# A graph network with four transformer layers on one core: three re-orderings around the gated feed-forward stage

## The chip, the cores and the metric

The kernel runs on one core of one Trainium2 chip. Its time is the device time of one execution in microseconds (us); three runs of the kernel before gave 2254.66, 2255.79 and 2258.05, with a median of 2255.79. The profile is that of one more execution. The engines are named as the profile names them: PE (TensorE, with PEld for its weight loads), DVE (VectorE), ACT (ScalarE), POOL (GpSimd) and SP (SyncE, which here issues nearly all DMAs).

## The reference

Node features of 1024 rows by 512 are normalised, passed through a graph convolution, then through four layers of cross attention and a gated feed-forward block, then a second graph convolution. The change touches the feed-forward block alone:

```python
for i in range(L):                                    # L = 4
    a = _attn(_ln(h, ln2_w[i], ln2_b[i]), cond, Wq[i], Wk[i], Wv[i], Wo[i])
    h = h + a
    u = _ln(h, ln3_w[i], ln3_b[i]) @ geglu_w[i] + geglu_b[i]   # 512 -> 4096
    val, gate = jnp.split(u, 2, axis=-1)
    f = val * jax.nn.gelu(gate, approximate=False)             # 1024 x 2048
    h = h + f @ ffo_w[i] + ffo_b[i]                            # 2048 -> 512
h = _gcn(h, src, dst, gcn_out_w, gcn_out_b, n)
return h + x_in
```

## The kernel before

**Numbers in three parts.** [...] A product is then three matmuls for each block of 128 along the inner size: high by high, low by low, and third by third. The high and low products go into a PSUM bank, which is scaled by 1 + TINY, and the third product is added; in the chunks and in `Twelve` an ACT operation scales the bank in place (`g L373`, `g L1157`) between the first two and the third, so a unit has a `begin` (high, low, scaling) and an `end` (third), and other units' matmuls are put between the two.

**The gated block.** f transposed has 2048 rows in sixteen column blocks ("chunks") of 128. The normalised input is kept transposed in the tiles ln3T. The first two columns (`PLAIN = 2`) are computed as plain products in two halves of the rows (`halves`, class `Half`, L1028): the first half while the last attention group is finished, the second half, `half_1(0) + half_1(1)`, at L1891 and below. The other fourteen chunks use seven products of half the size in the place of eight (class `Chunk`, L1093): sums of blocks of the input ("late rows", held in `right`, numbered 5, 6, 4, 3) and sums of blocks of the weight. The late rows are split by the generator `late_parts` (L1871), whose steps the function `fill` takes: for a row first two ACT multiplications (L1863, one for each half of the row), then two steps with two DVE operations each (L1866, L1868). Row 5, 4 and 3 come from the tiles ln3S, row 6 from ln3T. The third step of a row also begins the next row, so the first `fill(3)` goes as far as row 6's multiplications and the second one as far as row 4's first pair of DVE operations.

**The chunk loop.** For each chunk the generator `Chunk.steps` (L1182) emits the products 0, 5, 6, 4, 1, 3, 2 and the additions between them; the endings of products 1, 3 and 2, the gates (ACT, L1172) and the two products of value and gate (DVE, L1223 and L1225) are put in the next chunk's iteration. Beside the chunk in work, the next one's weight blocks are summed on POOL (L1115), and split on ACT, DVE and POOL (L1081, L1082, L1087), and a later one is loaded by SP (L1105). f goes to DRAM (`f_dram`, L1267).

**The output.** `Output` (L1271) multiplies f by ffo_w in two halves of the rows and eight units (`UNITS`) of 256 inner rows each, sixteen units in all, of 24 matmuls (L1322): for four row blocks, two high by high, two low by low (bank fy) and two third by third (bank fx). `fetch(n)` loads a unit's f again and `split(n)` splits it (ah_f L304, al_f L305, as_f L310). `fetch_w(u)` loads a block of ffo_w, and `ahead` is a generator over the splits of all blocks, five steps each: one ACT multiplication (bh_wff, L1296), then for each half of the block a low part (bl_wff, L1299) and a third (bs_wff, L1303) on DVE. In the chunk loop, with n = 0 for the first chunk of the third group of four and n = 7 for the last chunk, the first block is fetched at n = -1 and split in five steps at n = 0 to 4. Each pass of the output loop fetches a unit and a block further on, splits the next unit's f, takes five steps of `ahead`, and emits its own unit's matmuls.

**What sets the order.** The kernel is traced in program order, and a scheduler orders each engine's instructions ahead of the run by its own estimate of times. `pin` keeps the instructions that it is given in program order on their engine, `in_order(engine)` does so for all in a block, and `behind_traced(engine)` ties each instruction of a block behind the last one traced on that engine. At run time each engine takes its instructions in the order thus fixed, and SP its DMAs. A new tile of a pool takes a free buffer; the pool `slots`, from which splits, weights and f come, has 35.

Of the kernel before, what the change touches and what calls it, by code (L numbers as in the profile page):

```python
# [26 lines left out]
def gnn_kernel(  # L27
# [68 lines left out]
    @contextmanager  # L96
    def in_order(engine):

        traced = nc.cur_bb.bb.instructions
        n = len(traced)  # L100
        before = next((i for i in reversed(traced) if i.engine == engine), None)
        yield
        for i in traced[n:]:
            if i.engine == engine:
                if before is not None:
                    tc.add_manual_dep(i, before.name, mybir.DependencyInfo(
                        mybir.DependencyClass.NoSync, mybir.DependencyReason.DATA))
                before = i

    @contextmanager  # L110
    def behind_traced(*engines):

        traced = nc.cur_bb.bb.instructions
        n = len(traced)
        last = {e: next(i for i in reversed(traced) if i.engine == e) for e in engines}
        yield
        for i in traced[n:]:
            if i.engine in last:
                tc.add_manual_dep(i, last[i.engine].name, mybir.DependencyInfo(
                    mybir.DependencyClass.NoSync, mybir.DependencyReason.DATA))  # L120

    def bank(name):
        return psum.tile([P, 512], F32, tag="bank", name=name)
# [168 lines left out]
    def twelve_bits(t):  # L292
        return t.bitcast(F32R)
# [709 lines left out]
    class HalfWeights:  # L1003
# [6 lines left out]
        def load(self, j):  # L1010
            parts = slots_of(3, f"gp_{self.l}_{j}")
            for i, t in enumerate(parts):
                nc.sync.dma_start(self.tall(t), half_dram[j, :, :, i].rearrange("n p f -> p n f"))
            self.parts[j] = [self.tall(t) for t in parts]
# [256 lines left out]
    class Output:  # L1271
# [37 lines left out]
            for u in range(UNITS):  # L1309
                yield from self.split_w(u)  # L1310

        def unit(self, n):

            s, u = divmod(n, UNITS)
            left, right = self.f.pop(n), self.w[u]
            for b in range(4):
                if u == 0:
                    self.banks[b] = [bank(f"{x}_{self.l}_{s}_{b}") for x in ("fy", "fx")]
                y, x = self.banks[b]
                for which, to in enumerate((y, y, x)):  # L1320
                    for k in range(2):
                        pin(nc.tensor.matmul(  # L1322
                            to, twelve_bits(left[which][0])[:, k, b * P:(b + 1) * P],
                            twelve_bits(right[which])[:, k, :],
                            start=u == 0 and which != 1 and k == 0,
                            stop=u == UNITS - 1 and which != 0 and k == 1, skip_group_check=True))
                if u == UNITS - 1:
                    to = h[4 * s + b]
                    nc.vector.scalar_tensor_tensor(to, y, 1.0 + TINY, to, OP.mult, OP.add)
                    nc.vector.tensor_tensor(to, x, to, OP.add)  # L1330
# [164 lines left out]
    for l in range(L):  # L1495
# [147 lines left out]
        def add_bias(t, *blocks):  # L1643
            if not ffb:
                with waiting_for(scores.last, mybir.EngineType.SP):
                    ffb.append(load_row(ffo_b, l * D, f"ffb_{l}"))
            for nb in blocks:
                t.tensor_tensor(h[nb], h[nb], ffb[0], OP.add)
# [85 lines left out]
        def sum_chunk(n):  # L1734
            if n < len(ready):
                ready[n].sums()

        def begin_split(n, low, t=nc.gpsimd):
            flow = ready[n].split_steps(low, t) if n < len(ready) else iter(())
            next(flow, None)  # L1740
            return flow
# [76 lines left out]
        with in_order(mybir.EngineType.DVE):  # L1818
            units = half_0(0) + half_0(1)
            before = oT  # L1820
# [66 lines left out]
        def fill(n=1):  # L1887
            for _ in range(n):
                next(parts, None)
# [3 lines left out]
        ready[0].end_first()  # L1893
        fill(3)
        units[1].begin()
        units[0].end()
        fill(3)
        ready.append(StagedChunk(l, PLAIN + 1))
        units[2].begin()
        units[1].end()  # L1900
# [10 lines left out]
        def split_rest(short, behind=None):  # L1911
            long = begin_split(0, False)
            next(long, None)
            with waiting_for(behind or split_left.low, mybir.EngineType.Pool):
                for flow in short, long:
                    for _ in flow:
                        pass

        output = Output(l)
        ahead = output.ahead()  # L1920
        before, short = None, iter(())
        for r in range(R):
            f = Gated(l, r) if r else f_first
            for c in range(0 if r else PLAIN, KC):
                n = (r - R + 2) * KC + c
                if n == -1:
                    output.fetch_w(0)
                if (r, c) == (R - 1, KC - 2):
                    output.fetch(0)
                chunk = ready.pop(0)  # L1930
                flow = chunk.steps(lambda: sum_chunk(1)) if before else first_flow
                chunk.f = f
                if before:
                    next(flow)
                if 0 < n < 5:
                    next(ahead)
                for _ in islice(short, 2):
                    pass
                if before:
                    next(flow)  # L1940
                the_last = (r, c) == (R - 1, KC - 1)
                if before and r:
                    if not the_last:
                        split_rest(short)
                    load()
                for _ in parts:
                    pass
                if the_last:
                    with in_order(mybir.EngineType.Activation), in_order(mybir.EngineType.DVE), \
                            in_order(mybir.EngineType.Pool):  # L1950
                        output.split(0, nc.gpsimd, lambda: split_rest(short, left_parts.low))
                    output.fetch(1)
                for step in range(3):
                    if before:
                        next(before, None)
                    next(flow)
                    if before and not r and step == 0:
                        split_rest(short)
                        load()
                    if step == 2 and not before:  # L1960
                        with in_order(mybir.EngineType.DVE):
                            add_bias(nc.vector, NG - 2, NG - 1)
                    if step == 1 and not before:
                        ready[0].load_rest()
                        sum_chunk(1)
                        load()
                        with tc.issue_after(ready[-1].loaded.ins):
                            for n in range(PLAIN):
                                f_first.store(n, (1,))
                before = flow  # L1970
                short = begin_split(0, True) if r or c > PLAIN else iter(())
                if n == 0:
                    next(ahead)
        output.fetch_w(1)
        output.fetch_w(2)
        for _ in range(3):
            next(before, None)

        def nothing():
            pass  # L1980
# [22 lines left out]
        else:  # L2003
# [11 lines left out]
            def split_of(to, raw, name, i):  # L2015
                for part, t in zip(to, right_parts(raw[i:i + 1], f"{name}_{l + 1}_{i}")):
                    part.extend(t)
# [16 lines left out]
        with in_order(mybir.EngineType.DVE):  # L2034
            for n in range(2 * UNITS):
                output.fetch(n + 2)
                output.split(n + 1)
                output.fetch_w(n + 3)
                for _ in range(5):
                    next(ahead, None)  # L2040
                output.unit(n)
                beside.get(n, nothing)()
            if not last:
                split_of(wv, raw_wv, "wv", 1)
# [80 lines left out]
```

## Time and profile before

| what | value |
|---|---|
| time, median of three runs | 2255.79 us |
| the profiled execution's own time | 2254.72 us |
| span of the profile | 2252.9 us |
| instructions | 35754 |
| granted TensorE clock | 1.0 |
| busy: PE / DVE / ACT / POOL | 2232.4 / 1718.0 / 1157.8 / 500.5 us |
| moved by DMA | 340.84 MB, mean 151 GB/s |

A busy time is the union of an engine's instructions; as matmuls overlap, a PE that is busy all the time need not run at its full pace. A line of the timeline has its start and duration in us, the engine, the line of the code, the operation, the tile written and those read, shapes, how many equal instructions are merged in it, and in brackets how long the engine had been idle and what released it. In tile names, gr, gl and gs are parts of the late rows (or rights), gha, gla, gsa and ghb, glb, gsb those of a chunk's weights, g the banks. SPq is the queue of SP.

### The profile page before, as it was taken

The numbers are of one execution on the slowest core, as the hardware profiler recorded it, in microseconds if no ns is written. First come the engines' busy times: TensorE is split into PE (matmuls) and PEld (weight loads), VectorE is DVE, ScalarE is ACT, GpSimd is POOL, SyncE is SP. The second block draws the span as 40 slices with busy tenths as digits, with TensorE's granted clock in tenths as the row PEclk, the third lists the DMA queues.
The fourth block names the chain that finished last, engine by engine and source line by source line (L and its number), as shares of the span: only waits on it lengthen the run. The fifth ranks groups of instructions, "written<-read, shape, count | busy, mean of one in ns | idle before, by whom it ended". The sixth has DMA issues, their size and how long they took to land. (4 is left out here: it accounts for less than half of the span.)

```text
span 2252.9 us, 35754 instructions
## 1 busy us (share of the span) xinstructions
PE 2232.4 (99%) x12768; PEld 1805.2 (80%) x12768; DVE 1718.0 (76%) x3300; ACT 1157.8 (51%) x2313; POOL 500.5 (22%) x483
## 2 busy tenths in 40 slices
PE   8999999999999999999999999999999999999999
PEld 4678888887888888888888888888888888888787
DVE  9886677999965567899976466889976466899965
ACT  7555555565354445565346445565436445565521
POOL 1122211386000000287000000178100000068201
PEclk9999999999999999999999999999999999999999
DMA  6154565434425265442534265443543346353551
GB/s 173 58 187 169 189 217 172 144 122 145 165 84 197 99 227 174 150 126 97 196 122 157 106 219 193 132 136 99 187 159 136 127 165 213 110 168 113 187 182 53
DMA packets 216953, 340.84 MB, mean 151 GB/s; under 512 B 16488, under 2 KB 117168, under 8 KB 216768
## 3 DMA queue, kind: packets, MB, share of 16 engines
q1 hardware_dynamic: 214672, 333.05, 43.5%
q0 software_dynamic: 1376, 4.30, 0.6%
q8 instruction: 105, 1.72, 0.3%
q10 hardware_dynamic: 720, 1.11, 0.1%
q14 instruction: 80, 0.66, 0.1%
HBM read 236.69 MB, written 101.72 MB: 150 GB/s over the span
## 5 line engine op out<-in xcount | busy, mean ns | idle before, releaser
L1157 ACT ACTIVATE g<-g 128x512 f32<-128x512 f32 x224 | 131.3, 586 | 183.9 <-PE g L1143 181.9
L1615 POOL TENSOR_TENSOR ln3T<-ln3T,ln3T 128x512 f32<-128x512 f32 x8 | 13.2, 1654 | 875.2 <-DVE ln3S L1608 875.2
L1322 PE MATMUL fx<-bs_wff,as_f 128*128 128x512 f32 x512 | 158.7, 390 | 0.0
L1322 PE MATMUL fy<-bl_wff,al_f 128*128 128x512 f32 x512 | 158.7, 390 | 0.0
L1322 PE MATMUL fy<-bh_wff,ah_f 128*128 128x512 f32 x512 | 157.7, 389 | 0.0
L304 ACT ACTIVATE ah_f<-fr 128x1024 fp32r<-128x1024 f32 x64 | 67.8, 1060 | 172.5 <-DVE al_f L305 80.4
L373 ACT ACTIVATE k<-k 128x512 f32<-128x512 f32 x125 | 73.1, 586 | 153.6 <-PE k L362 153.6
L832 DVE TENSOR_REDUCE nmax<-sc 128x2 f32<-128x512 f32 x128 | 83.7, 678 | 79.6 <-PE sc L823 79.5
L843 ACT ACTIVATE pr<-sc,nmax 128x256 f32<-128x256 f32 x256 | 118.4, 473 | 41.0 <-DVE nmax L832 40.9
L373 ACT ACTIVATE v<-v 128x512 f32<-128x512 f32 x127 | 74.8, 589 | 115.8 <-PE v L362 115.6
L1087 POOL TENSOR_TENSOR gsa<-gha,gla 128x512 fp32r<-128x512 f32 x96 | 122.5, 1299 | 21.4 <-DVE gla L1082 21.4
L1143 PE MATMUL g<-gr,gha 128*128 128x512 f32 x384 | 118.3, 389 | 0.0
L1322 PEld LDWEIGHTS fy<-bl_wff,al_f 128*128 128x128 f32 x512 | 96.1, 188 | 21.5 <-DVE bl_wff L1299 1.7
L1322 PEld LDWEIGHTS fx<-bs_wff,as_f 128*128 128x128 f32 x512 | 96.1, 188 | 21.4 <-DVE bs_wff L1303 1.7
L1322 PEld LDWEIGHTS fy<-bh_wff,ah_f 128*128 128x128 f32 x512 | 96.1, 188 | 19.9
L362 PE MATMUL v<-bh_wv,ch 128*128 128x512 f32 x384 | 106.7, 399 | 0.0
L362 PE MATMUL k<-ch,bh_wk 128*128 128x512 f32 x384 | 104.0, 393 | 0.0
L305 DVE SCALAR_TENSOR_TENSOR al_f<-ah_f,fr 128x1024 fp32r<-128x1024 f32 x64 | 78.1, 1221 | 33.6 <-ACT ah_f L304 27.5
L362 PE MATMUL v<-bl_wv,cl 128*128 128x512 f32 x384 | 103.1, 390 | 0.0
L362 PE MATMUL v<-bs_wv,cs 128*128 128x512 f32 x384 | 103.0, 391 | 0.0
L362 PE MATMUL k<-cl,bl_wk 128*128 128x512 f32 x384 | 102.8, 389 | 0.0
L362 PE MATMUL k<-cs,bs_wk 128*128 128x512 f32 x384 | 101.4, 395 | 0.0
(334 smaller groups left out, 5938.0 us busy)
## 6 DMA issues: line engine op xcount, KB each, us to landing
f_dram<-fT SPq DMA_DIRECT2D x128, 256.0 KB, 2.1
fr<-f_dram SPq DMA_DIRECT2D x64, 512.0 KB, 4.6
ch<-cond_dram SPq DMA_DIRECT2D x48, 512.0 KB, 4.8
cl<-cond_dram SPq DMA_DIRECT2D x48, 512.0 KB, 6.4
cs<-cond_dram SPq DMA_DIRECT2D x48, 512.0 KB, 7.5
chunk_dram<-gs SPq DMA_DIRECT2D x56, 384.0 KB, 2.5
wff<-in_L_gnn_ffo_w_dram SPq DMA_DIRECT2D x32, 512.0 KB, 5.0
half_dram<-gs SPq DMA_DIRECT2D x32, 384.0 KB, 3.5
```

The costliest lines, as they stand in the source:

```text
L304: nc.scalar.mul(twelve_bits(h), x, INWARD * TINY)
L305: left_parts.low = nc.vector.scalar_tensor_tensor(twelve_bits(l), h, -1.0 / TINY, x, OP.mult, OP.add)
L362: pin(nc.tensor.matmul(self.bank, twelve_bits(left[k // 2])[:, k % 2, self.c * P:(self.c + 1) * P], twelve_bits(right[k // 2])[:, k % 2, : ...
L373: nc.scalar.mul(self.bank, self.bank, 1.0 + TINY)
L832: nc.vector.tensor_reduce(nmax[u], banks[u].rearrange("p (a m) -> p a m", a=2), AX.X, OP.max, negate=True)
L843: nc.scalar.activation(pr3[:, a, :], ps3[:, a, :], AF.Exp, bias=nmax[u][:, a:a + 1], accum_out=tot[:, a:a + 1])
L1087: split_left.last = pin(t.tensor_tensor(s_at, h_at, l_at, OP.subtract))
L1143: pin(nc.tensor.matmul(to, self.part(i, which)[:, k, :], self.rights[i][which].bitcast(F32R)[:, k, :], start=start and k == 0, stop=stop a ...
L1157: pin(nc.scalar.mul(to, to, 1.0 + TINY))
L1322: pin(nc.tensor.matmul(to, twelve_bits(left[which][0])[:, k, b * P:(b + 1) * P], twelve_bits(right[which])[:, k, :], start=u == 0 and whic ...
L1615: t.tensor_tensor(b12, b22, b12, OP.subtract)
```

## The change

There are three edits. First, the second `fill(3)` of the late rows is traced before the ending of the second half's first unit, and its ACT instructions are tied behind the last ACT instruction traced before, the scaling of unit 1. Second, the second block of ffo_w is fetched at n = 4, and three of its five steps of splitting are taken at n = 5, 6 and 7; the output loop then always is three steps further in `ahead`. Third, `unit` becomes a generator `products` that stops twice in its first row block, and of unit 0 the high and the low products of the first row block (four matmuls) are emitted after the last chunk's ending of product 1 and before its endings of products 3 and 2.

```diff
--- before.py
+++ after.py
@@ -1309,7 +1309,7 @@
             for u in range(UNITS):
                 yield from self.split_w(u)
 
-        def unit(self, n):
+        def products(self, n):
 
             s, u = divmod(n, UNITS)
             left, right = self.f.pop(n), self.w[u]
@@ -1318,6 +1318,8 @@
                     self.banks[b] = [bank(f"{x}_{self.l}_{s}_{b}") for x in ("fy", "fx")]
                 y, x = self.banks[b]
                 for which, to in enumerate((y, y, x)):
+                    if which:
+                        yield
                     for k in range(2):
                         pin(nc.tensor.matmul(
                             to, twelve_bits(left[which][0])[:, k, b * P:(b + 1) * P],
@@ -1893,8 +1895,9 @@
         ready[0].end_first()
         fill(3)
         units[1].begin()
+        with behind_traced(mybir.EngineType.Activation):
+            fill(3)
         units[0].end()
-        fill(3)
         ready.append(StagedChunk(l, PLAIN + 1))
         units[2].begin()
         units[1].end()
@@ -1925,6 +1928,8 @@
                 n = (r - R + 2) * KC + c
                 if n == -1:
                     output.fetch_w(0)
+                if n == 4:
+                    output.fetch_w(1)
                 if (r, c) == (R - 1, KC - 2):
                     output.fetch(0)
                 chunk = ready.pop(0)
@@ -1932,7 +1937,7 @@
                 chunk.f = f
                 if before:
                     next(flow)
-                if 0 < n < 5:
+                if 0 < n < 8:
                     next(ahead)
                 for _ in islice(short, 2):
                     pass
@@ -1971,10 +1976,13 @@
                 short = begin_split(0, True) if r or c > PLAIN else iter(())
                 if n == 0:
                     next(ahead)
-        output.fetch_w(1)
         output.fetch_w(2)
-        for _ in range(3):
-            next(before, None)
+        next(before)
+        first_unit = output.products(0)
+        for _ in range(2):
+            next(first_unit)
+        for _ in before:
+            pass
 
         def nothing():
             pass
@@ -2038,7 +2046,8 @@
                 output.fetch_w(n + 3)
                 for _ in range(5):
                     next(ahead, None)
-                output.unit(n)
+                for _ in output.products(n) if n else first_unit:
+                    pass
                 beside.get(n, nothing)()
             if not last:
                 split_of(wv, raw_wv, "wv", 1)
```

## The prediction

> **What bounds the kernel.** I read the busy times on the page first, then what the weight loads of the matrix engine waited for, then the order of work by engine around each of those waits. The page's row of the matrix engine:
>
> ```profile
> PE 2232.4 (99%) x12768; PEld 1805.2 (80%) x12768; DVE 1718.0 (76%) x3300; ACT 1157.8 (51%) x2313; POOL 500.5 (22%) x483
> ```
>
> The matrix engine is never free, so an edit pays only where the stream of matmuls halts. From the list of waits of its weight loads (us in total, times, longest) these rows belong to places that the diff touches:
>
> ```profile
> PEld g L1028 <- ACT g L373: 2.3, 4, 0.6
> ...
> PEld g L1143 <- DVE g L1163: 2.0, 4, 0.7
> ...
> PEld fx L1322 <- DVE bs_wff L1303: 1.7, 4, 0.4
> PEld fy L1322 <- DVE bl_wff L1299: 1.7, 4, 0.4
> ```
>
> Each comes four times, once in each layer, so the first layer (with the timeline's columns start, duration, what, count, idle before it) may stand for all. The idle figure overstates the loss, since a load normally runs ahead of its matmul; I take the loss from the matmuls' starts. Place one, the second half's first products, at the late rows' splits:
>
> ```profile
> 411.77 4.70 PE L1028 MATMUL g<-gr,gp 128*128 128x512 f32 x20
> 416.62 0.73 PE L1028 MATMUL g<-gr,gp 128*128 128x512 f32 x2 [0.15 <-ACT g L373]
> 412.02 1.74 POOL L1615 TENSOR_TENSOR ln3T<-ln3T,ln3T 128x512 f32<-128x512 f32 x1 [4.54 <-DVE ln3S L1608]
> 414.41 0.63 ACT L1863 ACTIVATE gr<-ln3S 128x512 fp32r<-128x512 f32 x1 [0.57 <-DVE ln3S L1610]
> 414.95 1.13 ACT L1863 ACTIVATE gr<-ln3T 128x512 fp32r<-128x512 f32 x2
> 415.99 0.58 ACT L373 ACTIVATE g<-g 128x512 f32<-128x512 f32 x1
> ...
> 418.63 0.58 ACT L373 ACTIVATE g<-g 128x512 f32<-128x512 f32 x1
> ```
>
> Places two and three, the end of the last gated chunk and the start of the output's second unit (zero of my clock below is 552.15):
>
> ```profile
> 552.15 1.38 PE L1143 MATMUL g<-gr,gsb 128*128 128x512 f32 x4
> 553.49 0.71 PE L1143 MATMUL g<-gr,gs 128*128 128x512 f32 x2
> 554.04 0.62 PE L1322 MATMUL fy<-bh_wff,ah_f 128*128 128x512 f32 x2
> 559.49 0.61 PE L1322 MATMUL fy<-bh_wff,ah_f 128*128 128x512 f32 x2
> 559.94 0.88 PE L1322 MATMUL fy<-bl_wff,al_f 128*128 128x512 f32 x2
> 560.66 0.89 PE L1322 MATMUL fx<-bs_wff,as_f 128*128 128x512 f32 x2
> 561.39 0.40 PE L1322 MATMUL fy<-bh_wff,ah_f 128*128 128x512 f32 x1
> 552.06 1.29 DVE L1163 SCALAR_TENSOR_TENSOR g<-g,gu 128x512 f32<-128x512 f32 x2
> 555.85 1.23 DVE L305 SCALAR_TENSOR_TENSOR al_f<-ah_f,fr 128x1024 fp32r<-128x1024 f32 x1
> 557.11 1.23 DVE L310 TENSOR_TENSOR as_f<-ah_f,al_f 128x1024 fp32r<-128x1024 f32 x1
> 558.25 0.69 DVE L1299 SCALAR_TENSOR_TENSOR bl_wff<-wff,bh_wff 128x512 fp32r<-128x512 f32 x1
> ...
> 559.58 0.69 DVE L1299 SCALAR_TENSOR_TENSOR bl_wff<-wff,bh_wff 128x512 fp32r<-128x512 f32 x1
> 560.30 0.69 DVE L1303 SCALAR_TENSOR_TENSOR bs_wff<-bh_wff,bl_wff 128x512 fp32r<-128x512 f32 x1
> 553.57 1.30 ACT L1172 ACTIVATE g<-g,gcols 128x512 f32<-128x512 f32 x2 [4.29 <-PE g L1143]
> 554.77 1.05 ACT L304 ACTIVATE ah_f<-fr 128x1024 fp32r<-128x1024 f32 x1
> 555.72 1.05 ACT L1296 ACTIVATE bh_wff<-wff 128x1024 fp32r<-128x1024 f32 x1
> ```
>
> The pace: two matmuls take 0.61 (559.49), twenty 4.70 (411.77), so eighteen more take 4.09, 0.227 each. Place one: the twenty-first was due at 411.77 + 20 x 0.227 = 416.31, came at 416.62, and its pair took 0.73 instead of 0.61: 0.43 lost. Place two: six matmuls from 552.15 to 554.04 took 1.89 instead of 1.36: 0.53 lost. Place three: six from 559.49 to 561.39 took 1.90: 0.54 lost. The four places two include one with a longer wait (longest 0.7, the other three 0.43 on average), so I add 0.2 once, rounding its excess down. In all 4 x 1.50 + 0.2 = 6.2 us, 0.27% of the span, is the most that the three edits can gain where they stand.
>
> **Part one, late rows' high parts.** Nothing is added; two ACT multiplications for row 4 (the third row in order) and four DVE operations are traced earlier, the ACT ones tied behind the scaling of the second unit. In the trace the ACT took one piece that reads ln3S (414.41, a row other than the second, since the second reads ln3T) ahead of the second row's pair and of the scaling at 415.99 that the halted matmul wants. The first row's pair came before it, so by the order of the code it is row 4's first piece. It also sat idle 0.57 for it, from 413.84. With it tied back, the pair can start when the POOL sum that it reads ends, 412.02 + 1.74 = 413.76: so 413.84 to 414.97, then the scaling until 415.55, before the 416.31 at which it is wanted. The loss of 0.43 goes. What is late next? The scaling at 418.63 ended 4.80 after 414.41; the same ACT work without the idle 0.57 ends at 418.64. It is wanted twelve matmuls after 416.31, at 419.03: no new halt. DVE gets row 4's high part at the same time or sooner, and POOL and SP carry nothing of this part. Bounds: 0 if the second row's pair was not ready before 414.95, where it ran (then 414.95 + 1.13 + 0.58 = 416.66, no gain), 0.43 else. I take 0.43, because the POOL row puts the data at 413.76.
>
> Does the gain survive the thirteen chunks after it? These rows show how the chunk loop starts, how its ACT and DVE stand late in it, and the windows with POOL's first three sums of an iteration (us of the window, POOL busy), with and without a split of output weights on DVE:
>
> ```profile
> 431.06 0.58 ACT L1157 ACTIVATE g<-g 128x512 f32<-128x512 f32 x1 [0.32 <-PE g L1143]
> 432.63 1.22 DVE L1082 SCALAR_TENSOR_TENSOR gla<-gha,gxa 128x1024 fp32r<-128x1024 f32 x1 [0.72 <-ACT gha L1081]
> 525.04 0.58 ACT L1157 ACTIVATE g<-g 128x512 f32<-128x512 f32 x1 [0.32 <-PE g L1143]
> 526.72 1.06 ACT L1081 ACTIVATE gha<-gxa 128x1024 fp32r<-128x1024 f32 x1 [1.10 <-POOL gxa L1115]
> 515.19 1.02 DVE L1303 SCALAR_TENSOR_TENSOR bs_wff<-bh_wff,bl_wff 128x512 fp32r<-128x512 f32 x1
> 537.48 1.22 DVE L1082 SCALAR_TENSOR_TENSOR gla<-gha,gxa 128x1024 fp32r<-128x1024 f32 x1 [0.85 <-ACT gha L1081]
> 514.00:516.87 2.87, 2.64 (x3) 1.00 0.48 138
> 523.90:526.76 2.86, 2.61 (x3) 1.00 0.40 149
> ```
>
> Late in the stage the splits of the next chunk run as a circle of POOL, ACT and DVE (at 526.72 ACT waits 1.10 for POOL). But the circle starts behind PE: at 431.06 ACT waited for PE, and at 432.63 DVE waited 0.72 for ACT, more than the 0.43 by which PE would come sooner. So the circle shifts along, and the gain is kept.
>
> **Part two, output weights' second block.** One DMA of 512 KB moves four iterations forward on SP, past the stores, fetches and loads of those iterations; the pair of weight fetches after the last chunk becomes one. One ACT operation (1.05) goes into iteration n = 5, one DVE operation each into n = 6 and n = 7; the block's other two DVE operations stay in the output loop. Costs in the chunks: at n = 5 ACT has 1.10 idle before 526.72, which covers the 1.05, and the scaling at 525.04 slides by at most that. If this cover were gone, 1.05 would reach the matmuls in each layer. The DVE operation costs 1.02 beside POOL (515.19) against 0.69 alone (560.30). At n = 6 it falls into the 0.85 idle before 537.48, and 0.17 is left over, which nobody feels because no further chunk's split follows; uncovered it would be 1.02. At n = 7 there is no chunk to split, and the first output operand's split is what follows it. Bounds 0 to 1.02 each; I take 0. [...]
>
> The gain in unit 1: see part three, since both meet there.
>
> **Part three, first output products in the last chunk.** Four matmuls that were the unit's first now stand between the chunk's first ending pair and the two pairs that wait for L1163. No work is added. On my clock: pair at 0, four products 0.45 to 1.36, next pair at 1.36 (its L1163 is done at half of 1.29, that is 0.56), last pair at 1.81 (the second L1163 done at 1.20), and ten matmuls end at 2.27 without a halt. So 0.53 is gained. Their operands are ready: from 552.06 on DVE splits only what the second unit reads.
>
> The price: the pair that the gates at 553.57 wait for ended at 552.15 + 1.38 = 553.53; now it starts at 1.36 and ends one spacing and one matmul (0.39, from 0.61 - 0.227 rounded up) later, 1.98. The gates go from 1.42 to 2.02, 0.60 later, and with them the whole ACT and DVE queue behind: ah_f, al_f, as_f, and the first weight operation, 6.10 before, starts at 6.70. That is now the second half of bl_wff, until 7.39, and bs_wff follows 0.72 later (559.58 to 560.30), until 8.11. Unit 1 starts at 2.27 + 20 x 0.227 = 6.81 instead of 7.34 and wants them as its fourth and sixth matmul, at 7.49 and 7.95. Before, the sixth (561.39 - 0.227 = 561.16) started 0.17 after bs_wff's end, 560.99; so now at 8.28, and 0.33 of the old 0.54 stays. Part two thus gains 0.21 (bounds 0 and 0.54). Part two without part three would have gained it all: they compete for DVE.
>
> **The sum.** Per layer 0.43 + 0.21 + 0.53 = 1.17, four times 4.7, with the 0.2 of the longer wait 4.9 us. The profiled execution took 2254.72 (span 2252.9): 2249.8 after. That execution lies 1.07 below the median 2255.79, so for a median I say 2250.9.
>
> **Rivals.** First: part one gives nothing, because the second row's pair is not ready earlier or the chunk circle does not shift along: 1.7 less gain, 2252.6. For it: the pair ran at 414.95 and no row shows it ready before; against it: POOL's end at 413.76.
>
> Second: unit 1 does not halt at all, if ACT takes ah_f before the late gates while it is idle (4.29 before 553.57) and DVE's queue closes up: 4 x 0.33 = 1.3 more, 2249.6. Against it: it was idle there before, and did not.
>
> [...]
>
> Fourth, on the other side: ACT at n = 5 stands before the block's high part because its DMA has not landed; behind it on ACT wait the chunk's scalings and the next chunk's high part, and for those the matmuls. The fetch rows on SP and the time to landing (min, median, max):
>
> ```profile
> 462.43 0.43 SPq L1290 DMA_DIRECT2D wff<-in_L_gnn_ffo_w_dram  x1
> 521.97 0.37 SPq L1281 DMA_DIRECT2D fr<-f_dram  x1
> DMA to landing us min/median/max: 3.7/5.0/9.4
> ```
>
> If the fetch queues behind the stores like the one at 521.97, it lands at 527.0; the ACT would want it right ahead of 525.04. Then bh_wff ends at 528.05, the scaling at 528.6, and the high part ends at 529.7 instead of 527.78: 1.9 late per layer, 7.6 in all, against the gain of 4.9: 2258.5. It decides from 1.2 late per layer, that is a landing after 526.3. The same happens if no tile is free for the block (four more of the 35 are held). Against it: the first block's fetch, written at the top of its iteration just so, went out at 462.43 between stores, ahead of its iteration, and here that leaves some ten us.
>
> **How the numbers follow.** Forecast 0.50, first rival 0.23, second 0.12, third 0.07, fourth 0.08. A measurement of this kernel can tell about 0.2%, 4.5 us, from no change: below 2251.3 is faster. The forecast lies just below it, its remaining halt in unit 1 may be anything from 0.1 to 0.54, so I count 0.31 of its 0.50 as faster, with nearly all of the second rival and a little of the first: 0.44. Slower by over 0.2%, above 2260.3, is only the fourth with a later landing or something unseen: 0.06. The rest, 0.50, is within 0.2%. The range runs from the second rival less a us, 2248.5, over the first and the third to 2255.3; the fourth is left out.
>
> **What would show it.** Right: the wait on L373 at L1028 and the one on L1163 at L1143 gone from the list; that on bl_wff nearly gone, that on bs_wff left at about half; four products of fy ahead of the chunk's last pairs; a fetch of weights at about 511 and L1296 near 525 without waiting. Wrong: ACT L373 still behind ln3T's pair until 416.6; a new wait for a later L373; the PE's waits for ACT L1157 in the chunks longer than before; L1296 waiting for a DMA; or an al_f that starts later than 4.30 on my clock.

## The result and the profile after

The changed kernel takes 2252.32 us (median of 22 runs, 2251.43 to 2255.87), the kernel before 2255.39 beside it (22 runs): a ratio of 0.9987, with a 95% interval from 0.9981 to 0.9993. That is 3.1 us faster, 0.13%: a real gain that stays within the 0.2% the prediction called no change. Forecast were 2250.9 and a gain of 4.9; the time that came is that of the first rival, 2252.6, in which part one gives nothing. The profiled execution took 2252.54, with a span of 2250.8, against 2254.72 and 2252.9. The page's busy times, after:

```profile
PE 2230.2 (99%) x12768; PEld 1805.5 (80%) x12768; DVE 1720.7 (76%) x3300; ACT 1157.7 (51%) x2313; POOL 501.5 (22%) x483
```

The matrix engine has the same 12768 matmuls and is busy 2.2 us less. The waits of its weight loads, after (us in total, times, longest):

```profile
PEld g L1143 <- ACT g L1157: 3.8, 12, 0.4
PEld g L1028 <- ACT g L373: 2.3, 4, 0.6
PEld fx L1324 <- DVE bs_wff L1303: 1.7, 4, 0.4
PEld fy L1324 <- DVE bl_wff L1299: 0.8, 4, 0.2
...
PEld g L1143 <- DVE g L1163: 0.5, 2, 0.2
```

Of the four rows that the prediction started from, two stand as they stood: the wait of L1028 for the scaling L373, 2.3 in four, which part one was to remove, and the one for bs_wff, 1.7, which was forecast at about half. The one for bl_wff, forecast as nearly gone, has gone to half (1.7 to 0.8). The one for L1163 is gone from the chunk's end in all four layers; the 0.5 left in its row, in two, falls earlier in the chunk stage of the first and the fourth layer, where the kernel before had none. Lines below L1321 are numbered two higher than before.

**Place one** in the first layer, timeline of the kernel after (columns as in the prediction):

```profile
412.22 4.70 PE L1028 MATMUL g<-gr,gp 128*128 128x512 f32 x20
417.07 3.26 PE L1028 MATMUL g<-gr,gp 128*128 128x512 f32 x13 [0.16 <-ACT g L373]
...
414.87 0.63 ACT L1865 ACTIVATE gr<-ln3S 128x512 fp32r<-128x512 f32 x1 [0.57 <-DVE ln3S L1612]
415.40 1.13 ACT L1865 ACTIVATE gr<-ln3T 128x512 fp32r<-128x512 f32 x2
416.44 0.58 ACT L373 ACTIVATE g<-g 128x512 f32<-128x512 f32 x1
...
417.52 1.66 ACT L1865 ACTIVATE gr<-ln3S 128x512 fp32r<-128x512 f32 x3
```

The twenty-first matmul was due at 412.22 + 20 x 0.227 = 416.76 and came at 417.07: late by 0.31, as before. ACT still takes one piece of ln3S ahead of the second row's pair, still 0.57 idle before it, and the scaling L373 still stands third. The piece that the prediction wanted behind the scaling has not moved.

**Places two and three** in the first layer, after:

```profile
552.74 0.62 PE L1143 MATMUL g<-gr,gsb 128*128 128x512 f32 x2
553.19 0.62 PE L1324 MATMUL fy<-bh_wff,ah_f 128*128 128x512 f32 x2
...
554.57 0.62 PE L1143 MATMUL g<-gr,gs 128*128 128x512 f32 x2
555.02 0.61 PE L1324 MATMUL fx<-bs_wff,as_f 128*128 128x512 f32 x2
...
559.56 0.62 PE L1324 MATMUL fy<-bh_wff,ah_f 128*128 128x512 f32 x2
...
560.52 0.89 PE L1324 MATMUL fx<-bs_wff,as_f 128*128 128x512 f32 x2
561.25 0.63 PE L1324 MATMUL fy<-bh_wff,ah_f 128*128 128x512 f32 x2
...
554.77 1.30 ACT L1172 ACTIVATE g<-g,gcols 128x512 f32<-128x512 f32 x2 [4.90 <-PE g L1143]
555.49 0.75 DVE L1223 SCALAR_TENSOR_TENSOR fT<-g,gcols,g 128x512 f32<-128x512 f32 x1 [1.55 <-ACT g L1172]
...
557.05 1.23 DVE L305 SCALAR_TENSOR_TENSOR al_f<-ah_f,fr 128x1024 fp32r<-128x1024 f32 x1
559.45 0.68 DVE L1299 SCALAR_TENSOR_TENSOR bl_wff<-wff,bh_wff 128x512 fp32r<-128x512 f32 x1
560.17 0.69 DVE L1303 SCALAR_TENSOR_TENSOR bs_wff<-bh_wff,bl_wff 128x512 fp32r<-128x512 f32 x1
```

The prediction's clock has its zero here at 552.74. Ten matmuls from there end at 555.02, in 2.28 (forecast 2.27): the halt of 0.53 is gone. In unit 1 the next six, from 559.56 to 561.25, take 1.69 instead of 1.36: 0.33 lost of the old 0.54.

**The chunks** in which part two puts its fetch and three splits, after:

```profile
511.47 0.38 SPq L1290 DMA_DIRECT2D wff<-in_L_gnn_ffo_w_dram  x1
...
524.72 0.58 ACT L1157 ACTIVATE g<-g 128x512 f32<-128x512 f32 x1 [2.74 <-PE g L1143]
525.22 1.05 ACT L1296 ACTIVATE bh_wff<-wff 128x1024 fp32r<-128x1024 f32 x1
...
527.30 1.06 ACT L1081 ACTIVATE gha<-gxa 128x1024 fp32r<-128x1024 f32 x1 [0.54 <-POOL gxa L1115]
...
535.47 0.88 DVE L1299 SCALAR_TENSOR_TENSOR bl_wff<-wff,bh_wff 128x512 fp32r<-128x512 f32 x1
536.28 1.22 DVE L1082 SCALAR_TENSOR_TENSOR glb<-ghb,gxb 128x512 fp32r<-128x512 f32 x1
...
538.31 1.21 DVE L1082 SCALAR_TENSOR_TENSOR gla<-gha,gxa 128x1024 fp32r<-128x1024 f32 x1
545.15 0.68 DVE L1303 SCALAR_TENSOR_TENSOR bs_wff<-bh_wff,bl_wff 128x512 fp32r<-128x512 f32 x1
...
535.06 1.89 POOL L1115 TENSOR_TENSOR gxa<-gxa 128x256 f32<-128x256 f32 x2
537.03 1.07 POOL L1115 TENSOR_TENSOR gy<-gxb,gxa 128x256 f32<-128x256 f32 x1
```

The block's ACT operation follows the scaling without waiting for its DMA, which went out 13.75 earlier. The DVE operation of n = 6 takes 0.88, the split glb behind it 1.22 where it took 0.87 before (at 534.89), and together they use up the idle time that gla had. The wait of the chunks' matmuls for L1157 is 3.8 in twelve, against 3.7 before. From place one's first matmul to the zero of the prediction's clock the first layer takes 140.52, and took 140.38 before; over the four layers it is 0.44 more. The change run again has 0.27 more and part two alone 0.08 more, while part one alone, whose instructions are those of the kernel before, has 0.13 less. So the chunks gave back a few tenths of a us in all at most, and that much is not shown to come from the edits.

### The profile page after: what moved, and what is told of

It is laid out like the page before. It is cut to its first block, busy times and chain, and to the rows that moved or that the text cites. A ratio compares the mean times of both kernels' runs of the same rounds, so it can differ in the third digit from the quotient of the medians.

```text
span 2250.8 us, 35743 instructions
## 1 busy us (share of the span) xinstructions
PE 2230.2 (99%) x12768; PEld 1805.5 (80%) x12768; DVE 1720.7 (76%) x3300; ACT 1157.7 (51%) x2313; POOL 501.5 (22%) x483
## 5 line engine op out<-in xcount | busy, mean ns | idle before, releaser
L1157 ACT ACTIVATE g<-g 128x512 f32<-128x512 f32 x224 | 131.4, 586 | 182.3 <-PE g L1143 179.6
L373 ACT ACTIVATE k<-k 128x512 f32<-128x512 f32 x125 | 73.1, 586 | 151.7 <-PE k L362 151.5
L373 ACT ACTIVATE v<-v 128x512 f32<-128x512 f32 x127 | 74.8, 589 | 117.0 <-PE v L362 117.0
```

The source lines that it names most:

```text
L373: nc.scalar.mul(self.bank, self.bank, 1.0 + TINY)
L1157: pin(nc.scalar.mul(to, to, 1.0 + TINY))
```

## The experiments

Each was timed in five rounds, eleven runs, beside the kernel before on the same chip (33 runs in each of two sets). The table has the medians of all runs, and beside them the medians of those runs whose mean granted clock is 1.000 on record; the last section takes up the others.

| kernel | median | ratio to before, 95% interval | median at clock 1.000 (runs) |
|---|---|---|---|
| before, first set | 2255.64 | | 2255.12 (24) |
| part one alone | 2255.46 | 1.0000 (0.9991 to 1.0009) | 2255.16 (8) |
| part two alone | 2253.11 | 0.9992 (0.9983 to 1.0001) | 2252.79 (7) |
| part three alone | 2257.46 | 1.0011 (1.0002 to 1.0020) | 2257.19 (8) |
| the change again | 2252.91 | 0.9988 (0.9979 to 0.9997) | 2252.31 (6) |
| before, second set | 2255.11 | | 2254.99 (28) |
| the change without part one | 2252.69 | 0.9990 (0.9981 to 0.9999) | 2252.18 (6) |
| the change, row 3 tied as well | 2250.88 | 0.9983 (0.9974 to 0.9992) | 2250.58 (9) |
| the change, block's rest in the gap | 2250.98 | 0.9980 (0.9971 to 0.9989) | 2250.96 (10) |
| both of these | 2250.28 | 0.9978 (0.9969 to 0.9987) | 2249.55 (6) |

**Part one alone.** The kernel before with this edit and no other.

```diff
         units[1].begin()
+        with behind_traced(mybir.EngineType.Activation):
+            fill(3)
         units[0].end()
-        fill(3)
```

> The kernel before with part one alone. Theory A: the ACT piece that stands before the scaling belongs to row 3 and not to row 4, so tying row 4 changes no engine's order; the time is that of the kernel before, within 0.3 us, and the wait of L1028 for L373 stays at 2.3 us in four. Theory B (the forecast's): row 4's piece goes behind the scaling, and 1.7 us are gained.

Measured: a ratio of 1.0000. The wait in its profile is the one of before to the digit:

```profile
PEld g L1028 <- ACT g L373: 2.3, 4, 0.6
```

In the program as built, the instructions of all five engines, with the tiles that they read and write, stand in the same order as before, and so do their waits: the edit changes no instruction's place. The full tile names there also say what the piece at 414.41 is: the first half of row 3, the last row, which the scheduler had drawn ahead by itself; the three pieces of ln3S behind the scaling (417.52 above) are row 3's other half and row 4's two. Row 4's pair stood behind the scaling before the change already. Part one moves in the code what the schedule had moved on its own.

**The change without part one.**

```diff
         units[1].begin()
-        with behind_traced(mybir.EngineType.Activation):
-            fill(3)
         units[0].end()
+        fill(3)
```

> The changed kernel without part one, that is parts two and three. Theory A: the same as the changed kernel, 3.1 us less than before, within 0.3 us. Theory B: 0.4 us or more slower than the changed kernel.

Measured: 2252.69, the changed kernel's time (2252.32, and 2252.91 when run again). Its order is that of the changed kernel, instruction for instruction. So nothing of part one works only beside the others either.

**Row 3 tied as well.** If the piece is row 3's first half, tying that row has to remove the halt.

```diff
         units[2].begin()
         units[1].end()
-        fill(1)
+        with behind_traced(mybir.EngineType.Activation):
+            fill(1)
```

> The changed kernel with row 3's two ACT multiplications also tied behind the ACT instruction last traced. Theory A: the scaling that PE waits for at L1028 then comes right behind row 5's pair, the halt of 0.43 goes in each layer, and PE's lead is kept through the chunks: 1.7 us less than the changed kernel. Theory B: the chunks' circle of POOL, ACT and DVE does not start sooner, the halts late in the chunk stage grow by as much, and the time is that of the changed kernel within 0.4 us.

Measured: 2250.88, 1.8 less than without part one (1.6 at clock 1.000). The place in its first layer, timeline (this execution is about 3 us later here):

```profile
415.35 8.32 PE L1028 MATMUL g<-gr,gp 128*128 128x512 f32 x36
...
416.27 1.15 ACT L1865 ACTIVATE gr<-ln3S 128x512 fp32r<-128x512 f32 x2
417.36 0.58 ACT L373 ACTIVATE g<-g 128x512 f32<-128x512 f32 x1
417.86 1.15 ACT L1865 ACTIVATE gr<-ln3T 128x512 fp32r<-128x512 f32 x2
...
420.08 0.58 ACT L373 ACTIVATE g<-g 128x512 f32<-128x512 f32 x1 [0.50 <-PE g L1028]
420.57 2.18 ACT L1865 ACTIVATE gr<-ln3S 128x512 fp32r<-128x512 f32 x4
```

Thirty-six matmuls run through without a halt, the wait of L1028 for L373 is gone from the list, and the four pieces of rows 4 and 3 stand together behind the second scaling. The twenty-third matmul starts 4.99 after the first, against 5.41 in the changed kernel; in each layer it comes 0.42 to 0.44 sooner, against the 0.43 worked out in the prediction, and the matmuls stay sooner through the thirteen chunks. So its price for the halt and its step on the chunk circle were right; only the edit that it credited with them was the wrong one.

**Part two alone**, with the output begun as before.

```diff
+                if n == 4:
+                    output.fetch_w(1)
...
-                if 0 < n < 5:
+                if 0 < n < 8:
                     next(ahead)
...
-        output.fetch_w(1)
```

> The kernel before with part two alone. Theory A: unit 1 finds both late weight parts done and its halt of 0.54 goes in each layer: 2.2 us less than before; the last chunk's halt for L1163 stays. Theory B: the splits at n = 5 to 7 cost the chunks as much as unit 1 gains: within 0.5 us of before.

Measured: 2.5 less than before by the medians, 2.3 at clock 1.000. The interval just reaches 1, but the seven runs at clock 1.000, the slowest 2253.50, all lie below the fastest of the kernel before, 2254.12. The waits for bl_wff and bs_wff are gone from its list; what is left of the four places, beside the wait of L1028 that stays 2.3:

```profile
PEld g L1143 <- DVE g L1163: 1.9, 4, 0.5
```

Unit 1's six matmuls take 1.36 in each layer, so its whole 0.54 is gained when part three is absent.

**Part three alone**, the generator `products` and what follows, with the weights' second block split as before.

```diff
-        for _ in range(3):
-            next(before, None)
+        next(before)
+        first_unit = output.products(0)
+        for _ in range(2):
+            next(first_unit)
+        for _ in before:
+            pass
```

> The kernel before with part three alone, the second block of weights split where it was. Theory A: the gates and the DVE queue behind them come 0.60 later and unit 1 starts 0.53 sooner, so the halt in unit 1 grows from 0.54 to 1.66 and each layer is 0.59 longer, less the 0.2 of the one longer wait: 2.2 us slower than before. Theory B: DVE makes up for it, and 2.3 us are gained.

Measured: 1.8 slower than before by the medians, 2.1 at clock 1.000; the interval lies above 1. Its waits, and unit 1 in the first layer:

```profile
PEld fy L1324 <- DVE bl_wff L1299: 6.3, 8, 1.1
```

```profile
559.07 0.61 PE L1324 MATMUL fy<-bh_wff,ah_f 128*128 128x512 f32 x2
559.71 0.49 PE L1324 MATMUL fy<-bl_wff,al_f 128*128 128x512 f32 x1
561.03 0.50 PE L1324 MATMUL fy<-bl_wff,al_f 128*128 128x512 f32 x1 [0.83 <-DVE bl_wff L1299]
561.37 0.89 PE L1324 MATMUL fx<-bs_wff,as_f 128*128 128x512 f32 x2
562.10 0.63 PE L1324 MATMUL fy<-bh_wff,ah_f 128*128 128x512 f32 x2
```

The chunk's end gains 0.52 here too (the wait for L1163 shrinks to 0.2, once). But the gates and the DVE queue behind them come 0.61 later (2.03 on the prediction's clock, 1.42 before) while PE comes sooner, so unit 1's six matmuls take 562.10 - 559.07 = 3.03 instead of 1.36: 1.67 lost where before lost 0.54. The edit moved a halt and made it larger. With part two, which takes half of DVE's work out of that place, the same edit no longer loses, but it adds little: the change is 0.2 below part two alone by the medians of this set, 0.5 at clock 1.000, since 0.33 of the 0.52 is lost again in unit 1.

**The change again** stood beside these four, as the mark for them.

> The changed kernel itself, for comparison on the same chip: 3.1 us less than before, as in the result. Were parts two and three independent, it would be the sum of the two runs with one part each; by theory A it is not, as part three alone loses.

Measured: 2252.91, a ratio of 0.9988, which holds the first result.

**The block's rest in the gap.** In the changed kernel DVE stands idle 1.55 for the last gates (555.49 above), while two splits of the second block are still to come. Here these two are traced after the first four output products, ahead of the gates' products.

```diff
         for _ in range(2):
             next(first_unit)
+        for _ in range(2):
+            next(ahead)
         for _ in before:
             pass
```

> The changed kernel with the second block's last two DVE operations moved ahead of the last chunk's two products of value and gate, where DVE was idle for 1.55 us and they need 1.37. Theory A: they cost nothing there and the halt of 0.3 left in unit 1 goes in each layer: 1.2 us less than the changed kernel. Theory B: another operand is late next, such as the f parts or the third block's weights, and less than 0.4 us is gained.

Measured: 2250.98, 1.7 less than the change without part one (1.2 at clock 1.000, as expected). DVE at the place in its first layer (this execution is 2.4 later here):

```profile
556.27 0.68 DVE L1299 SCALAR_TENSOR_TENSOR bl_wff<-wff,bh_wff 128x512 fp32r<-128x512 f32 x1
556.98 0.69 DVE L1303 SCALAR_TENSOR_TENSOR bs_wff<-bh_wff,bl_wff 128x512 fp32r<-128x512 f32 x1
557.91 0.75 DVE L1223 SCALAR_TENSOR_TENSOR fT<-g,gcols,g 128x512 f32<-128x512 f32 x1 [0.24 <-ACT g L1172]
```

Both splits fit, with 0.24 of idle time left; the gates' product is no later for it, and the waits for bl_wff and bs_wff are gone. The 0.33 that the prediction left in unit 1 was a matter of order on DVE, not of its load.

**Both of these in the change.**

> Both of the edits of the two runs before this one in the changed kernel. If they are independent and each does what theory A says: 2.9 us less than the changed kernel, about 6 less than before.

Measured: 2250.28, a ratio of 0.9978 (0.9969 to 0.9987) to the kernel before, the fastest of all; at clock 1.000 it is 2.6 below the change without part one, where 2.9 was expected, and 5.4 below before (4.8 by the medians). The two gains nearly add up (1.6 and 1.2). A small wait shows in its list, 1.2 in all, none of it at a chunk's end: 0.9, two of its four, falls into the fourth layer, and 0.2 each into the first and the third. What brings it is open; the kernel with part one alone has two such waits too, 0.4 in all, with the instructions of the kernel before.

```profile
PEld g L1143 <- DVE g L1163: 1.2, 4, 0.6
```

## Why the prediction was right and where it was wrong

**Part one: wrong, in one step.** "The first row's pair came before it, so by the order of the code it is row 4's first piece." It is row 3's. The order of the code does not settle which piece it is, since the scheduler may draw a later row's operation ahead where nothing pins it, and row 4 and row 3 read the same tile name, ln3S. The row itself had a hint that was passed over: the idle 0.57 ended with a DVE write of ln3S (L1610), so the piece was the one whose input was written last. The prediction's own sign of being wrong, L373 still behind ln3T's pair until 416.6, came: it ended at 417.02, and this layer runs 0.45 later after the change. As all that followed hung on this, the term of 0.43 a layer, 1.7 us, fell out. Its size, the reason why it halts, that nothing else is late next, and its way through the chunk circle were borne out by tying row 3, though there ACT takes the scaling ahead of the second row's pair, and not behind it.

**Part three: right.** Forecast on the prediction's clock, then measured: ten matmuls 2.27 and 2.28; gates 2.02 and 2.03; al_f 4.30 and 4.31; first weight operation 6.70 and 6.71; unit 1 6.81 and 6.82.

**Part two: right.** bs_wff was to end at 8.11 and ended at 560.86 - 552.74 = 8.12; 0.33 of the halt was to stay, and 0.33 stayed. The rows in the list of waits did not follow it: bl_wff's was to be nearly gone and came to half, bs_wff's was to halve and did not move. That it would have gained all 0.54 without part three, and that the two compete for DVE, the two kernels with one part each show: 2.5 faster and 1.8 slower alone, 2.7 faster together in the same set. The prediction's words missed how strongly: without part two, part three is a loss. Costs in the chunks were forecast as nothing, and the few tenths above are the most that show. At n = 6 the idle time before gla was to shrink from 0.85 with 0.17 of delay left over; gla has none left, and comes 538.31 - 537.48 - 0.59 = 0.24 later against the shift of the whole execution.

**The sum.** Without part one it is 4 x 0.74 + 0.2 = 3.2 us; measured were 3.1 by medians, and, when run again, 2.8 at clock 1.000. The likeliest time missed by the one term. That the range holds the time is owed to the other two and to the first rival, whose time was right by luck.

**The rivals.** The first gave the time, though by a reason that it did not name: it had the pair not ready or the circle in the way, and the pair was ready, as the kernel with row 3 tied shows: ACT takes it right behind the scaling, at 417.86, which is 2.51 after the first of the thirty-six matmuls, and 3.18 in the kernel before. That the edit does nothing at all, because the schedule already has it, should have stood among the rivals. The second fell: ACT stood idle 4.90 and ah_f stayed behind the gates. The third, with 0.07 of the chances and a place in the range, put a delay on POOL at n = 6. That delay was the author's estimate, and no run shows it: the prediction's two windows have POOL busy for 2.64 and 2.61, with and without a split on DVE beside it, and in the changed kernel POOL's two sums at 535.06 take 1.89, and two such sums took 1.89 before at 534.46, and the high part that waits for them comes at 536.98 instead of 536.38, which is the shift of the whole execution. DVE paid, 0.88 against 0.68 at 545.15, and 1.22 against 0.87 for glb. POOL's last sum, which that high part does not read, took 1.07 at 537.03 against 0.80 at 536.43. Neither stood still for the other's whole length: the DVE operations were lengthened by 0.20 and 0.35, one of POOL's sums by 0.27. The fourth fell: L1296 at 525.22 waited for no DMA.

## What to carry to other kernels

Before an edit is credited with moving an operation, find out which operation the row in the trace is: a tile name shared by several buffers and the order of the code do not say it, when a scheduler fixes the order; an edit that leaves that order as it was can be told without a run. Work earlier for one engine is worth what the queue of the next allows: part three alone lost 2 us, and gained 0.2 to 0.5 with the edit that made room on DVE. And when a halt remains, look for idle time just before it on the engine that is late (1.55 on DVE here): moving the late work there gained the 1.2 that was left.

## What the runs showed of the hardware that was not expected

The granted clock of the matrix engine, 1.0 in the profiles of before and after, fell to one half for one stretch near the start in three of the ten profiled executions, each of another kernel. In windows of 3.41 us around it (the columns are the window, busy times and counts of PE, PEld, DVE, ACT and POOL, the granted clock, DMA share and rate), for the kernel with the block's rest in the gap:

```profile
83.72:87.13 3.41, 1.42 (x4) 0.68 (x4) 1.39 (x9) 0.59 (x1) 0.00 (x0) 1.00 0.04 10
87.14:90.55 3.41, 3.41 (x5) 1.35 (x4) 2.43 (x6) 2.56 (x4) 0.19 (x1) 0.50 0.14 1
90.56:93.97 3.41, 3.41 (x15) 2.64 (x14) 2.29 (x5) 2.78 (x5) 0.00 (x0) 1.00 0.02 5
```

and for the one with row 3 tied:

```profile
122.26:125.67 3.41, 1.19 (x6) 0.72 (x5) 2.98 (x5) 2.90 (x4) 0.00 (x0) 1.00 1.09 329
125.67:129.08 3.41, 3.41 (x9) 2.64 (x10) 2.98 (x13) 0.77 (x2) 1.02 (x1) 0.50 1.01 303
```

The stretch is 3.41 long each time, and in the 3.41 before it PE had been busy for only 1.42 and 1.19 (1.02 in the third execution, that of part one alone, in 122.25 to 125.66), since it waited for other engines there (1.99 for DVE, 2.22 for ACT). Eight matmuls of the first stretch took 5.37, from 85.78, and the same eight 3.67 in the changed kernel, from 85.45. How long PE is busy in the 3.41 just before does not decide alone. At the first of the two places the kernel with row 3 tied had PE busy for less, 1.16 of 3.41, and kept its clock:

```profile
83.70:87.11 3.41, 1.16 (x3) 0.49 (x3) 0.92 (x6) 0.58 (x1) 0.00 (x0) 1.00 0.04 10
```

Where such steps of the clock begin is an estimate from its record in the traces of before and after. The record holds 1.0 for 2239.143 us in before and for 2235.730 in after, ahead of a half clock at the end; the two are 3.413 apart, and are 656 and 655 times 3.4133. Counted back from 125.67, where the half clock of this execution begins, in steps of that length, the stretch just shown lies across two steps, and neither is as idle:

```profile
81.30:84.71 3.41, 2.31 (x7) 0.90 (x6) 0.49 (x2) 0.58 (x1) 0.00 (x0) 1.00 0.04 7
84.71:88.12 3.41, 1.79 (x4) 0.87 (x5) 1.76 (x11) 0.00 (x0) 0.00 (x0) 1.00 0.04 10
```

Counted from the start of the same record, at 14.09 and 13.84, PE is busy 1.68 or more in every step of before and 1.65 or more in every step of after, but for the last ones, ahead of the half clock, with 0.00 and 0.83. Where the line lies between the 1.42 above and 1.65 is open, and that PE's busy time is all that counts was not shown.

It matters for small differences. In the first set the runs of the kernel before at a mean clock of 0.999 have a median of 2256.97, those at 1.000 one of 2255.12. If they had such a stretch, as the three profiled executions at 0.999 had, a chance event in the first 130 us weighs 1.9 us, as much as one part of this change.
